# A two-layer graph attention kernel: loads, first products, copies and norms in other places at both ends

## The chip, the core and the metric

The kernel runs on one core of a Trainium2 chip. The metric is the device time of one execution in microseconds (us); less is better. TensorE (PE) multiplies, VectorE (DVE), ScalarE (ACT) and GpSimd (POOL) do the elementwise work, SyncE (SP) issues most of the DMAs. Each engine works through its own queue in order and waits on semaphores for the others.

## What is computed

The input `x` is 128 graphs of 128 nodes with 512 features, float32; `adj` is a boolean mask for each graph. Two layers follow each other, each a masked attention with a residual sum and a layer norm:

```python
# layer 0: 4 heads of 64
x = layernorm(x + attention(x @ Wq, x @ Wk, x @ Wv, mask=adj) @ Wo + bo)
# layer 1: 8 heads of 64, with a layer norm of its own ahead, the diagonal always allowed
h = (x - mean(x)) * rsqrt(var(x) + 1e-5) * gamma + beta
q, k, v = split(h @ w_qkv.T)
x = layernorm(x + attention(q, k, v, mask=adj | eye) @ w_out.T + b_out)
```

`attention` is softmax(q k' / 8, masked) v for each head.

## The kernel before

The 128 graphs are worked in 64 groups `g` of two. The whole program is unrolled, and the order of the source is the order of each engine's queue. `opening` loads and turns the weights and starts groups 0 and 1; `step(s)` for s = 2 to 63 works on several groups at once, layer 0 of group s beside layer 1 of groups s-3 to s-5; `closing_a` (s = 64), `closing_b(65)`, `closing_b(66)` and `last` (s = 67) empty this pipeline.

The matrix products are done by Strassen's scheme (Winograd's form): 2x2 blocks, seven products numbered 1 to 7, with sums of the blocks made beforehand. `sums` and `out_sums` (both through `halves_sums`, L323) make those of the activations on POOL with four subtractions or additions, `combine` (L206) those of the weights on DVE. Products 1, 6, 7, 4 accumulate in one PSUM bank `a`, 5 and 3 in `f`, 2 goes into `c`. In between, the bank is read: after 1, 5 and 6 by a copy on ACT ("tap", L369 and L499), after the others by an addition on DVE. So product 6 of a kind waits for the tap of 1, 7 for that of 6, 4 for the addition of 7.

- `product_0` (L461) makes q, k and v of layer 0 from `xT` and `w0`; `qk` and `v` (`product`, L331) those of layer 1; `out_product` (L507) the output projections, with their additions into the rows `R` at L532.
- Attention: `scores` (L544, part 0 for layer 0, parts 1 and 2 for the two graphs of layer 1), `masked` (L585, copies of the allowed scores into `SM` on DVE), `maxima` (L599), `exps` (L606, eight on ACT in two halves), `normalised` (L615, a reciprocal on DVE and a product on POOL), then the turn of the probabilities: `blocks` (L633) transposes 32x32 blocks on DVE and writes them to a scratch in DRAM, `probs_arrive` fetches them back into `pT` by four DMAs; `blocks_direct` (L654) turns them on PE instead. `attend` (L668) multiplies them with v and copies the result to `aT` on ACT. `cleared` (L578) fills `SM` with the masking value on POOL.
- Rows: `addend` (L706) adds the bias to `R` on POOL (for layer 1 after a scaling on ACT, L712), `stats` (L718) takes mean and variance on DVE, `roots` computes scale and shift on POOL and puts the norm itself into a list `later`; `flush()` emits what stands there: two ACTIVATEs (L758) and, for layer 1, the output DMA. `finish_direct` (L295) turns the rows for layer 1 on PE.
- `setup` is a list of weight turns (four PE transposes each and a copy to SBUF), filled by `load_transposed` and emitted by `prepare(n)`.
- At the very end `out_plain` makes the last two output rows, graph by graph, in plain products, each graph in a bank of its own with two halves; `norm_plain` adds, takes the statistics and normalises.

SP issues the loads in source order. Wq is loaded by ACT's queue, Wk and Wv by SP's, w_qkv and w_out last. In steps 3 and 4 the tap-free product 2 of v is put ahead of product 1 (L936).

Of the kernel before, what the change touches and what calls it, by code (L numbers as in the profile page):

```python
# [27 lines left out]
def kernel(ctx: ExitStack, tc: tile.TileContext, x, adj, wq, wk, wv, wo, bo,  # L28
# [87 lines left out]


    ident = const.tile([P, P], F32, name="ident")
    make_identity(nc, ident)
    eye = const.tile([P, P], U8, name="eye")  # L120
    nc.vector.tensor_copy(eye, ident)
    mhalf = const.tile([P, 4], F32, name="mhalf")
    nc.gpsimd.memset(mhalf, -0.5)


    HF = INNER[0] // 2
    w0 = const.tile([P, KC, 3, 2, HF], F32, name="w0")
    ws0 = const.tile([P, 3, KC // 2, 3, HF], F32, name="ws0")
# [20 lines left out]
    gb_raw = one.tile([2 * KC, P], F32, tag="sm2", name="gb_raw")  # L149
    gb = const.tile([P, 2 * KC], F32, name="gb")  # L150

    setup = []
    def load_transposed(dst, src, name):
        rows, cols = src.shape
        raws = []
        for r in range(rows // P):
            raw = spare.pop(0)
            nc.sync.dma_start(raw, src[r * P:(r + 1) * P, :])
            raws.append(raw)

        def part(r):
            raw = raws[r]
            pt = mm_tile(f"{name}t_{r}")
            for c in range(cols // P):
                nc.tensor.transpose(pt[:, c * P:(c + 1) * P], raw[:, c * P:(c + 1) * P], ident)
# [7 lines left out]
        setup.extend(lambda r=r: part(r) for r in range(rows // P))  # L173

    nc.sync.dma_start(gb_raw[:KC], gamma.rearrange("(c p) -> c p", p=P))
# [7 lines left out]


# [23 lines left out]
    def weight_sums_0():  # L208
        combine(*(w0[:, c:c + KH, :, h] for c in (0, KH) for h in range(2)), *(ws0[:, i] for i in range(3)))
# [85 lines left out]
    def finish_direct(g):  # L295
# [13 lines left out]
        sums(1, g)  # L309
# [21 lines left out]
    def product(kind, g, i, take=True):  # L331
# [17 lines left out]
        elif first:  # L349
            ACC[kind, which] = ps_st.tile([P, 512], F32, tag=which, name=f"{kind}{which}_{g}")  # L350
# [110 lines left out]
    def product_0(g, *which):  # L461
# [6 lines left out]
        for i in which:  # L468
# [4 lines left out]
            bank, first = INTO[i]  # L473
            if first and bank == "c":
# [14 lines left out]
            for n, (o, lhsT, rhs) in enumerate(todo):  # L489
                nc.tensor.matmul(o, lhsT, rhs, start=first and n == 0, stop=n == len(todo) - 1,  # L490
                                 skip_group_check=True)
            src = acc[:, :3 * P]
# [291 lines left out]
    def norm_plain(g, b):  # L784
        row = R[g][:, b]
        n = E // 2
        acc = ACC["op", b]
        st = two.tile([P, 2, nc.vector.BN_STATS_DIM], F32, tag="st_last", name=f"st_last{b}")
        for i in range(2):
            h = slice(i * n, (i + 1) * n)  # L790
            nc.vector.tensor_add(row[:, h], acc[:, h], row[:, h])
# [5 lines left out]
        nc.gpsimd.tensor_tensor(root, ve, mhalf[:, :1], op=ALU.pow)  # L797
        nc.vector.tensor_scalar(row, row, mv[:, 0:1], root, op0=ALU.subtract, op1=ALU.mult)
        nc.sync.dma_start(out[g * G + b], row)


# [13 lines left out]
    def opening():  # L815
# [4 lines left out]
        for h in range(2):  # L820
            nc.scalar.activation(w0[:, :, 0, h, :], w0[:, :, 0, h, :], AF.Copy, scale=SCALE)
        product_0(0, 1)
        weight_sums_0()
        product_0(0, 2, 5, 6, 3)
# [31 lines left out]
    def step(s):  # L856
# [26 lines left out]
        normalised(s, 0)  # L883
        out_product(0, s - 2, *(() if s == 2 else (6,)), 3)
        exps(s, 1, 0)
# [77 lines left out]
    def closing_a():  # L963
# [31 lines left out]
        blocks(s, 1)  # L995
        exps(s, 2, 1)
# [151 lines left out]
```

## Time and profile before

| | us |
|---|---|
| median of 3 runs | 2765.82 |
| lowest and highest | 2763.13, 2767.58 |
| the profiled execution | 2759.03 |
| its span, first to last instruction | 2757.3 |
| PE, DVE, ACT, POOL busy outside 200 to 2600 us | 328, 229, 169, 200 |

The profile is that of one execution. A line of its timeline has start, duration, engine, source line, operation, output and inputs, the shape and the number of merged records; in square brackets stand the idle time of the engine before it and what ended that. "issue" means a time in which an engine waited for nothing that is shown. A float32 matmul leaves two records. The lines of who waits for whom give the total, the number of waits and the longest. The granted TensorE clock was 0.999 over the execution.

### The profile page before, as it was taken

Reading aid. Unit: us, or ns where it says so; the run is one execution under the profiler, and the core shown is the slowest. Engines: PE = TensorE matmul, PEld = TensorE weight load, DVE = VectorE, ACT = ScalarE, POOL = GpSimd, SP = SyncE. Lnnn points to the kernel's source line nnn. Section 1 sums busy time; section 2 is a strip of 40 time slices with the busy share of each in tenths; the row PEclk is TensorE's granted clock in tenths of the full one; section 3 lists DMA queues with packets and bytes.
Section 4 is the critical chain, followed back from the end, with each engine's and each line's share of the span. In section 5 each row is a group of like instructions: output and inputs, shape, how many; then the busy total and the mean of one; then the engine's idle time right before and its main releaser. Section 6 shows DMA issues by size and latency. Waiting matters only on the chain.

```text
span 2757.3 us, 49223 instructions
## 1 busy us (share of the span) xinstructions
PE 2725.2 (99%) x15781; PEld 2024.6 (73%) x15781; DVE 2025.0 (73%) x3662; ACT 1510.6 (55%) x4805; POOL 1750.2 (63%) x2311
## 2 busy tenths in 40 slices
PE   8999999999999999999999999999999999999998
PEld 7867777677776677776776766777767767677787
DVE  5777777777777777777777777777777777777665
ACT  3465565564564655655645546556556465465554
POOL 4566666666666666666666666666666666666664
PEclk9999999999999999999999999999999999999999
DMA  6577878778778788787787787877877877878741
GB/s 171 151 196 211 220 205 222 209 205 225 214 202 227 202 215 218 206 220 213 202 228 209 208 224 203 218 212 207 225 207 207 225 206 214 219 204 222 204 126 62
DMA packets 525330, 562.73 MB, mean 204 GB/s; under 512 B 55304, under 2 KB 434192, under 8 KB 525072
## 3 DMA queue, kind: packets, MB, share of 16 engines
q1 hardware_dynamic: 524496, 559.05, 75.8%
q8 instruction: 127, 2.08, 0.3%
q14 instruction: 131, 1.07, 0.1%
q10 hardware_dynamic: 576, 0.52, 0.1%
HBM read 300.95 MB, written 258.47 MB: 203 GB/s over the span
## 4 chain that ended last, share of the span: by engine, by line
PE 89%; DMA 4%; ACT 3%; DVE 1%; POOL 1%; SPq 1%; issue 1%; ACTq 0%; POOLq 0%; DVEq 0%
PE qka L359 14%; PE a L490 11%; PE oa L528 11%; PE va L359 8%; PE qkf L359 7%; PE av L691 6%; PE of L528 6%; PE f L490 5%; PE vf L359 4%; PE qkc L359 4%; PE c L490 3%; PE oc L528 3%; PE sc L562 2%; PE sc L568 2%; PE vc L359 2%; DMA scrk<-tk 2%
## 5 line engine op out<-in xcount | busy, mean ns | idle before, releaser
L612 ACT ACTIVATE sm<-sm,nmax 128x128 f32<-128x128 f32 x1536 | 595.4, 393 | 7.6 <-DVE nmax L603 6.0
L621 POOL TENSOR_TENSOR sm<-sm,rec 128x1024 f32<-128x1024 f32 x192 | 364.1, 1896 | 360.5 <-DVE rec L620 357.6
L713 POOL TENSOR_TENSOR r<-r,bias 128x1024 f32<-128x1024 f32 x128 | 301.4, 2356 | 127.1 <-ACT r L712 127.1
L532 DVE TENSOR_TENSOR r<-oa,r 128x256 f32<-128x256 f32 x508 | 211.5, 416 | 159.8 <-PE oa L528 126.0
L612 ACT ACTIVATION_READ_ACCUMULATOR sm<-sm,nmax 128x1 f32 x1536 | 295.4, 192 | 0.0
L369 ACT COPY ev<-va 128x256 f32<-128x256 f32 x128 | 47.6, 372 | 442.9 <-PE va L359 442.9
L732 POOL TENSOR_SCALAR ve<-mv 128x2 f32<-128x2 f32 x191 | 41.4, 217 | 376.8 <-DVE mv L725 366.3
L639 DVE STREAM_TRANSPOSE turnedp<-sm 128x1024 f32<-128x1024 f32 x188 | 233.4, 1242 | 63.8 <-POOL sm L621 63.8
L758 ACT ACTIVATE r<-r,shift,root 128x512 f32<-128x512 f32 x254 | 192.8, 808 | 122.2 <-POOL shift L747 122.2
L603 DVE TENSOR_REDUCE nmax<-sm 128x8 f32<-128x1024 f32 x192 | 226.3, 1204 | 0.1
L359 PE MATMUL qkf<-w,xs 128*128 128x512 f32 x472 | 221.8, 592 | 0.0
L359 PE MATMUL qka<-wsqk,xs 128*128 128x512 f32 x472 | 221.8, 592 | 0.0
L528 PE MATMUL oa<-wso,so 128*128 128x256 f32 x760 | 206.1, 380 | 2.3 <-POOL so L323 1.8
L528 PE MATMUL of<-wo,so 128*128 128x256 f32 x760 | 206.0, 380 | 0.7 <-POOL so L323 0.4
L323 POOL TENSOR_TENSOR xs<-xT 128x256 f32<-128x256 f32 x256 | 188.3, 736 | 28.3 <-DVE xT L112 23.4
L490 PE MATMUL a<-ws,xs 128*128 128x128 f32 (+1 forms) x760 | 182.1, 375 | 0.0
L490 PE MATMUL f<-w,xs 128*128 128x128 f32 (+1 forms) x760 | 182.1, 375 | 0.0
L597 DVE COPY_PREDICATED sm<-m,sc 128x512 f32<-128x512 uint8 x256 | 172.5, 727 | 12.1 <-PE sc L562 3.6
L724 DVE BATCH_NORM_STATS2 st<-r 128x6 f32<-128x512 f32 x254 | 174.9, 688 | 2.3
L583 POOL MEMSET sm<- 128x1024 f32 x192 | 174.9, 952 | 0.0
L359 PEld LDWEIGHTS qka<-wsqk,xs 128*128 128x128 f32 x472 | 89.7, 190 | 112.9 <-issue 112.9
L359 PEld LDWEIGHTS qkf<-w,xs 128*128 128x128 f32 x472 | 89.7, 190 | 112.9 <-issue 112.9
(181 smaller groups left out, 6478.6 us busy)
## 6 DMA issues: line engine op xcount, KB each, us to landing
scrp<-turnedp SPq DMA_DIRECT2D x188, 512.0 KB, 3.2
pT<-scrp SPq DMA_DIRECT2D x252, 256.0 KB, 5.2
x<-in_x_dram SPq DMA_DIRECT2D x256, 128.0 KB, 5.0
r<-in_x_dram SPq DMA_DIRECT2D x64, 512.0 KB, 3.2
out_dram<-r SPq DMA_DIRECT2D x63, 512.0 KB, 4.3
scr<-turned SPq DMA_DIRECT2D x62, 512.0 KB, 4.7
raw<-scr SPq DMA_DIRECT2D x248, 128.0 KB, 4.1
pT<-scrp SPq DMA_DIRECT2D x248, 128.0 KB, 3.9
```

Source lines behind the costliest of these rows:

```text
L323: nc.gpsimd.tensor_tensor(o, a0, a1, op=op)
L359: nc.tensor.matmul(o, lhsT, rhs, start=first and m == 0, stop=m == len(todo) - 1, skip_group_check=True)
L490: nc.tensor.matmul(o, lhsT, rhs, start=first and n == 0, stop=n == len(todo) - 1, skip_group_check=True)
L528: nc.tensor.matmul(acc, left[:, c], right[:, c], start=first and c == 0, stop=c == hk - 1, skip_group_check=True)
L532: nc.vector.tensor_add(part, acc, part)
L583: nc.gpsimd.memset(sm, NEG1 if part else NEG0)
L603: nc.vector.tensor_reduce(NMAX[part], SM[part], AX.X, ALU.max, negate=True)
L612: nc.scalar.activation(sm[:, i, k, :], sm[:, i, k, :], AF.Exp, bias=nmax[:, i, k:k + 1], accum_out=total[:, i, k:k + 1])
L621: nc.gpsimd.tensor_tensor(SM[part], SM[part], rec[:, :, :, None].to_broadcast([P, 2, K1, N]), op=ALU.mult)
L639: nc.vector.transpose(t.rearrange("p q (h r) -> p q h r", r=32), SM.pop(part).rearrange("p i k (q r) -> p q (i k) r", r=32))
L713: nc.gpsimd.tensor_tensor(R[g], R[g], (bias0, bias1)[l][:, None, :].to_broadcast([P, G, E]), op=ALU.add)
L758: nc.scalar.activation(R[g][:, b], R[g][:, b], AF.Identity, bias=shift[:, b:b + 1], scale=root[:, b:b + 1])
```

## The change

The first loads: the loader of Wq, Wk, Wv is a function, with Wv now on ACT's queue; the `eye` copy is on ACT; the loads of w_qkv's rows stand ahead of and between those of group 1's `x`, the masks, rows, `wo` and the biases. Twelve matmuls of the identity with itself stand at the head of PE's queue. Wq is scaled on DVE, and products 1 and 2 of group 0 as well as the sums of its weights are done for q, k and v one after the other. In steps 3 and 4 product 1 of v has another bank (`a0`) and its old order, and `normalised(s, 0)` stands later. In the closing turns masks, copies, norms, turns of blocks and clearings stand in other places of the queues. At the end the additions, statistics and norms of the two last graphs are interleaved. Nothing in `step` changes for s above 4.

```diff
+    HF = INNER[0] // 2
...
+    def load_w0(i, queue):
+        for a in range(4):
+            queue.dma_start(w0[32 * a:32 * a + 32, :, i].rearrange("p c h f -> p c (h f)"),
+                            (wq, wk, wv)[i][a * P:(a + 1) * P].rearrange("(c i) f -> i c f", i=32))
+    load_w0(0, nc.scalar)
     ident = const.tile([P, P], F32, name="ident")
     make_identity(nc, ident)
     eye = const.tile([P, P], U8, name="eye")
-    nc.vector.tensor_copy(eye, ident)
+    nc.scalar.copy(eye, ident)
...
-    for i, w in enumerate((wq, wk, wv)):
-        for a in range(4):
-            (nc.sync if i else nc.scalar).dma_start(
-                w0[32 * a:32 * a + 32, :, i].rearrange("p c h f -> p c (h f)"),
-                w[a * P:(a + 1) * P].rearrange("(c i) f -> i c f", i=32))
-    load_mask(0)
-    load_rows(0)
-    load(1)
-    wo0 = const.tile([P, INNER[0] // P, E], F32, name="wo0")
-    nc.sync.dma_start(wo0, wo.rearrange("(c p) f -> p c f", p=P))
-    bias0 = const.tile([P, E], F32, name="bias0")
-    nc.sync.dma_start(bias0, bo[None, :].to_broadcast([P, E]))
-    bias1 = const.tile([P, E], F32, name="bias1")
-    nc.sync.dma_start(bias1, b_out[None, :].to_broadcast([P, E]))
-    transposed(0)
-    load_quarters(1)
+    load_w0(1, nc.sync)
+    load_w0(2, nc.scalar)
+    ready = mm_tile("ready")
+    for _ in range(12):
+        nc.tensor.matmul(ready[:, :P], ident, ident, start=True, stop=True, skip_group_check=True)
...
+    def load_transposed(dst, src, name, *which):
...
+        for r in which:
+            raw = spare.pop(0)
+            nc.sync.dma_start(raw, src[r * P:(r + 1) * P, :])
+            setup.append(lambda r=r, raw=raw: part(r, raw))
+    transposed(0)
+    load_transposed(w1, w_qkv, "w_qkv", 0, 1, 2, 3)
+    load_quarters(1)
+    load_mask(0)
+    load_transposed(w1, w_qkv, "w_qkv", 4, 5)
+    wo0 = const.tile([P, INNER[0] // P, E], F32, name="wo0")
+    nc.sync.dma_start(wo0, wo.rearrange("(c p) f -> p c f", p=P))
+    load_transposed(w1, w_qkv, "w_qkv", 6, 7, 8, 9)
+    load_rows(0)
+    bias0 = const.tile([P, E], F32, name="bias0")
+    nc.sync.dma_start(bias0, bo[None, :].to_broadcast([P, E]))
+    load_transposed(w1, w_qkv, "w_qkv", 10, 11)
...
+    setup.append(turn_gamma_beta)
+    load_transposed(wo1, w_out, "w_out", 0, 1, 2, 3)
+    setup.append(setup.pop(-3))
+    load(1)
+    bias1 = const.tile([P, E], F32, name="bias1")
+    nc.sync.dma_start(bias1, b_out[None, :].to_broadcast([P, E]))
...
-    def weight_sums_0():
-        combine(*(w0[:, c:c + KH, :, h] for c in (0, KH) for h in range(2)), *(ws0[:, i] for i in range(3)))
+    def weight_sums_0(t):
+        combine(*(w0[:, c:c + KH, t, h] for c in (0, KH) for h in range(2)), *(ws0[:, i, :, t] for i in range(3)))
...
-    load_transposed(w1, w_qkv, "w_qkv")
-    setup.append(turn_gamma_beta)
-    load_transposed(wo1, w_out, "w_out")
-    setup.append(setup.pop(-3))
...
-        sums(1, g)
...
         elif first:
-            ACC[kind, which] = ps_st.tile([P, 512], F32, tag=which, name=f"{kind}{which}_{g}")
+            own = kind == "v" and g < 2 and which == "a"
+            ACC[kind, which] = ps_st.tile([P, 512], F32, tag="a0" if own else which, name=f"{kind}{which}_{g}")
...
-    def product_0(g, *which):
+    def product_0(g, *which, ts=(0, 1, 2)):
...
             bank, first = INTO[i]
+            first = first and 0 in ts
...
             if g in PLAIN_0:
                 todo = [(parts[:, (t + odd) % 3], *((right[:, c, t], left[:, c]) if t < 2 else
                                                     (left[:, c], right[:, c, t])))
-                        for t in range(3) for c in range(KH)]
+                        for t in ts for c in range(KH)]
...
+            if 2 not in ts:
+                continue
...
-    def norm_plain(g, b):
-        row = R[g][:, b]
+    def add_plain(g, b, i):
         n = E // 2
-        acc = ACC["op", b]
-        st = two.tile([P, 2, nc.vector.BN_STATS_DIM], F32, tag="st_last", name=f"st_last{b}")
-        for i in range(2):
-            h = slice(i * n, (i + 1) * n)
-            nc.vector.tensor_add(row[:, h], acc[:, h], row[:, h])
-            nc.vector.bn_stats(st[:, i], row[:, h])
-        mv = two.tile([P, nc.vector.BN_AGGR_DIM], F32, tag="mv", name=f"mv_last{b}")
-        nc.vector.bn_aggr(mv, st)
+        h = slice(i * n, (i + 1) * n)
+        row = R[g][:, b, h]
+        if i == 0:
+            ST[b] = two.tile([P, 2, nc.vector.BN_STATS_DIM], F32, tag="st_last", name=f"st_last{b}")
+        nc.vector.tensor_add(row, ACC["op", b][:, h], row)
+        nc.vector.bn_stats(ST[b][:, i], row)
+        mv = MV["last", b] = two.tile([P, nc.vector.BN_AGGR_DIM], F32, tag="mv", name=f"mv_last{b}")
+        nc.vector.bn_aggr(mv, ST[b])
         ve, root = (two.tile([P, 1], F32, tag=t, name=f"{t}_last{b}") for t in ("ve1", "root1"))
         nc.gpsimd.tensor_scalar(ve, mv[:, 1:2], 1.0, EPS, op0=ALU.mult, op1=ALU.add)
         nc.gpsimd.tensor_tensor(root, ve, mhalf[:, :1], op=ALU.pow)
+        return root
+    def norm_plain(g, b, root):
+        row, mv = R[g][:, b], MV["last", b]
         nc.vector.tensor_scalar(row, row, mv[:, 0:1], root, op0=ALU.subtract, op1=ALU.mult)
         nc.sync.dma_start(out[g * G + b], row)
...
         for h in range(2):
-            nc.scalar.activation(w0[:, :, 0, h, :], w0[:, :, 0, h, :], AF.Copy, scale=SCALE)
-        product_0(0, 1)
-        weight_sums_0()
-        product_0(0, 2, 5, 6, 3)
+            nc.vector.tensor_scalar_mul(w0[:, :, 0, h, :], w0[:, :, 0, h, :], SCALE)
+        for t in range(3):
+            product_0(0, 1, 2, ts=(t,))
+            weight_sums_0(t)
+        product_0(0, 5, 6, 3)
...
-        normalised(s, 0)
+        if s not in (3, 4):
+            normalised(s, 0)
         out_product(0, s - 2, *(() if s == 2 else (6,)), 3)
+        if s in (3, 4):
+            normalised(s, 0)
...
-        if s in (3, 4):
-            second = product("v", s - 3, 2, take=False)
-            v(s - 3, 1)
-            second()
-        else:
-            v(s - 3, 1, 2)
+        v(s - 3, 1, 2)
...
         blocks(s, 1)
+        cleared(s + 1, 1)
         exps(s, 2, 1)
...
         stats(1, s - 5, 1)
-        cleared(s + 1, 1, 2)
+        cleared(s + 1, 2)
         with_self(s - 2)
-        blocks(s, 0)
-        probs_arrive(s, 0)
-        addend(0, s - 1)
-        addend(1, s - 4)
...
     def closing_b(s):
         made = scores(s, 1, 2)
-        masked(made, s, 1, 2)
+        masked(made, s, 1)
+        if s == NG + 1:
+            blocks(s - 1, 0)
+            probs_arrive(s - 1, 0)
+            addend(0, s - 2)
+            addend(1, s - 5)
+        maxima(s, 1)
         v(s - 4, 1, 2)
-        maxima(s, 1)
+        flush()
         v(s - 4, 6, 5)
         exps(s, 1, 0)
-        flush()
         v(s - 4, 7, 3)
-        maxima(s, 2)
+        masked(made, s, 2)
         v(s - 4, 4)
-        exps(s, 1, 1)
-        normalised(s, 1)
         attend(s, 1, 2)
         out_sums(1, s - 5)
-        blocks(s, 1)
+        exps(s, 1, 1)
+        maxima(s, 2)
         finish_direct(s - 3)
+        normalised(s, 1)
         out_product(1, s - 5, 1, 2)
         attend(s, 0)
         out_sums(0, s - 2)
         exps(s, 2, 0)
+        blocks(s, 1)
         out_product(1, s - 5, 5, 6)
+        sums(1, s - 3)
+        exps(s, 2, 1)
         qk(s - 3, 1)
-        exps(s, 2, 1)
+        normalised(s, 2)
         out_product(1, s - 5, 7, 3)
         qk(s - 3, 2)
-        normalised(s, 2)
         out_product(1, s - 5, 4)
-        qk(s - 3, 6)
         blocks(s, 2)
         probs_arrive(s, 1, 2)
+        cleared(s + 1, 1, 2)
+        qk(s - 3, 6)
         out_product(0, s - 2, 1, 2, 5)
         qk(s - 3, 5)
...
         out_product(0, s - 2, 7)
+        flush()
         qk(s - 3, 3)
         out_product(0, s - 2, 4)
-        cleared(s + 1, 1, 2)
         qk(s - 3, 4)
...
         out_plain(NG - 1, 1, 0, 1)
-        norm_plain(NG - 1, 0)
-        norm_plain(NG - 1, 1)
+        for i in range(2):
+            add_plain(NG - 1, 0, i)
+        root = root_plain(0)
+        add_plain(NG - 1, 1, 0)
+        norm_plain(NG - 1, 0, root)
+        add_plain(NG - 1, 1, 1)
+        norm_plain(NG - 1, 1, root_plain(1))
```

More of the change, by code (lines that the diff above doesn't have):

```diff
@@ L115 @@
     load_quarters(0)
+    HF = INNER[0] // 2
+    w0 = const.tile([P, KC, 3, 2, HF], F32, name="w0")
+    ws0 = const.tile([P, 3, KC // 2, 3, HF], F32, name="ws0")
+    def load_w0(i, queue):
[3 more added lines that the diff above has]
+    load_w0(0, nc.scalar)
     ident = const.tile([P, P], F32, name="ident")
@@ L120, with part @@
     eye = const.tile([P, P], U8, name="eye")
-    nc.vector.tensor_copy(eye, ident)
+    nc.scalar.copy(eye, ident)
     mhalf = const.tile([P, 4], F32, name="mhalf")
     nc.gpsimd.memset(mhalf, -0.5)
-    HF = INNER[0] // 2
-    w0 = const.tile([P, KC, 3, 2, HF], F32, name="w0")
-    ws0 = const.tile([P, 3, KC // 2, 3, HF], F32, name="ws0")
-    for i, w in enumerate((wq, wk, wv)):
-        for a in range(4):
-            (nc.sync if i else nc.scalar).dma_start(
-                w0[32 * a:32 * a + 32, :, i].rearrange("p c h f -> p c (h f)"),
-                w[a * P:(a + 1) * P].rearrange("(c i) f -> i c f", i=32))
-    load_mask(0)
-    load_rows(0)
-    load(1)
-    wo0 = const.tile([P, INNER[0] // P, E], F32, name="wo0")
-    nc.sync.dma_start(wo0, wo.rearrange("(c p) f -> p c f", p=P))
-    bias0 = const.tile([P, E], F32, name="bias0")
-    nc.sync.dma_start(bias0, bo[None, :].to_broadcast([P, E]))
-    bias1 = const.tile([P, E], F32, name="bias1")
-    nc.sync.dma_start(bias1, b_out[None, :].to_broadcast([P, E]))
-    transposed(0)
-    load_quarters(1)
+    load_w0(1, nc.sync)
[3 more added lines that the diff above has]
+        nc.tensor.matmul(ready[:, :P], ident, ident, start=True, stop=True, skip_group_check=True)
     w1 = const.tile([P, KC, 3 * INNER[1]], F32, name="w1")
     wo1 = const.tile([P, INNER[1] // P, E], F32, name="wo1")
-    gb_raw = one.tile([2 * KC, P], F32, tag="sm2", name="gb_raw")
-    gb = const.tile([P, 2 * KC], F32, name="gb")
     setup = []
[L153 to L162, printed above, removed]
+    def load_transposed(dst, src, name, *which):
+        def part(r, raw):
             pt = mm_tile(f"{name}t_{r}")
-            for c in range(cols // P):
+            for c in range(KC):
                 nc.tensor.transpose(pt[:, c * P:(c + 1) * P], raw[:, c * P:(c + 1) * P], ident)
@@ L171, in part @@
                 nc.vector.tensor_copy(to, pt)
-        setup.extend(lambda r=r: part(r) for r in range(rows // P))
+        for r in which:
[14 more added lines that the diff above has]
+    load_transposed(w1, w_qkv, "w_qkv", 10, 11)
+    gb_raw = one.tile([2 * KC, P], F32, tag="sm2", name="gb_raw")
+    gb = const.tile([P, 2 * KC], F32, name="gb")
     nc.sync.dma_start(gb_raw[:KC], gamma.rearrange("(c p) -> c p", p=P))
@@ L782, in out_plain, with root_plain @@
                                  stop=c == K1 - 1, skip_group_check=True)
[L784 to L785 removed]
+    def add_plain(g, b, i):
         n = E // 2
[L787 to L794 removed]
+        h = slice(i * n, (i + 1) * n)
[4 more added lines that the diff above has]
+        nc.vector.bn_stats(ST[b][:, i], row)
+    def root_plain(b):
+        mv = MV["last", b] = two.tile([P, nc.vector.BN_AGGR_DIM], F32, tag="mv", name=f"mv_last{b}")
+        nc.vector.bn_aggr(mv, ST[b])
         ve, root = (two.tile([P, 1], F32, tag=t, name=f"{t}_last{b}") for t in ("ve1", "root1"))
@@ L797, in norm_plain @@
         nc.gpsimd.tensor_tensor(root, ve, mhalf[:, :1], op=ALU.pow)
+        return root
+    def norm_plain(g, b, root):
+        row, mv = R[g][:, b], MV["last", b]
         nc.vector.tensor_scalar(row, row, mv[:, 0:1], root, op0=ALU.subtract, op1=ALU.mult)
         nc.sync.dma_start(out[g * G + b], row)
+    ST = {}
     def v(g, *which):
```

## The prediction

> **What bounds the kernel now.** I read the page first, then the busy time by stage, then who TensorE (PE) waits for at the two ends, then the timeline around each wait.
>
> ```profile
> span 2757.3 us, 49223 instructions
> ...
> PE 2725.2 (99%) x15781; PEld 2024.6 (73%) x15781; DVE 2025.0 (73%) x3662; ACT 1510.6 (55%) x4805; POOL 1750.2 (63%) x2311
> ```
>
> The reader is to see that PE is busy in all but 32.1 us of the span; no other engine passes 73%. The stages say where those 32 us are:
>
> ```profile
> 200.00:1000.00 800.00, 798.25 (x4493) 583.54 (x4492) 598.37 (x1082) 446.68 (x1424) 516.41 (x680) 1.00 0.80 213
> 1000.00:2600.00 1600.00, 1598.74 (x8964) 1165.71 (x8963) 1197.19 (x2162) 894.62 (x2849) 1033.88 (x1368) 1.00 0.80 213
> ```
>
> The first number after the length is PE's busy time: 3.0 us idle in 2400. The steady loop has nothing to give; all that can be had lies in the first 130 us and after 2600. PE's waits there, first of the opening, then of the closing:
>
> ```profile
> PE a L490 <- ACT w L821: 10.1, 1, 10.1
> PE w_qkvt L165 <- DMA raw_r<-in_L_gnn_w_qkv_dram: 1.5, 1, 1.5
> PE va L359 <- ACT ev L369: 1.0, 2, 0.5
> PE a L490 <- DMA w<-in_L_gnn_Wv_dram: 0.9, 1, 0.9
> PE oa L528 <- DVE r L532: 0.4, 1, 0.4
> ```
>
> ```profile
> PE oa L528 <- ACT aT L696: 2.7, 2, 1.6
> PE oa L528 <- POOL so L323: 1.8, 2, 1.1
> PE av L691 <- DMA pT<-scrp: 1.5, 1, 1.5
> PE qka L359 <- ACT xT L289: 1.0, 1, 1.0
> PE va L359 <- DVE v L384: 0.6, 1, 0.6
> PE of L528 <- POOL so L323: 0.4, 1, 0.4
> ```
>
> Each wait is short, so a fix is worth at most its own length. One loss hides inside "busy": the same eight records at 10 us and at 28 us.
>
> ```profile
> 10.07 2.08 PE L490 MATMUL a<-xT,w 128*128 128x128 f32 x8 [10.07 <-ACT w L821]
> 28.24 1.16 PE L490 MATMUL a<-xT,w 128*128 128x128 f32 x8
> ```
>
> 0.26 us a record against 0.13 (pitch 0.111: twelve start at 28.24 and the next product at 29.57). The first 24 records run from 10.07 to 16.36; at the later pitch they would take 2.7.
>
> [...] full speed comes near 15.7 us, 5.6 after the start; no row shows how long a warm array stays warm. [...] So I give Wv on ACT's queue no earlier arrival than the trace shows (issues at 6.95 to 8.8, last landing 12.8). [...] the first sum of `op_0` waits until the whole bank is written (the tail's rows below), not just its half.
>
> **Opening, in order of time.** x's last quarter lands near 8.3 (transposes start at 8.38 and end at 9.69), Wq at 8.04. Before, ACT loads its table (1.28) and scales half 0 by 10.0. After, the table load moves to the `eye` copy, beside the loads, and DVE scales behind the transposes: two TENSOR_SCALARs of 128x512, nearest row L798 at 0.55 (I bound it by 0.3 and 0.6). PE's start becomes 9.69 + 0.55 = 10.25, a loss of 0.2. The 12 identity matmuls are 24 records; from `ident` (1.3) at the cold 0.26 they end by 7.6, before x, and so cost nothing. They should leave the array warm[...].
>
> Products 1 and 2 now go in three parts of 8 records (0.89 warm). q: 10.25 to 11.15; k (Wk landed by 10.4): to 12.05; v waits for Wv, 13.0 to 13.9. DVE: the sums are four 128x256 subtractions for each part, 0.43 each by the L206 row, 1.72: q 10.8 to 12.5, k to 14.2, then product 2's addition (behind ACT's copy) to 15.2, v to 16.9 with its first result at 15.65. Product 5 does 8 records to 14.8, waits 0.85, ends at 16.1; products 6 and 3 at 1.33 each end at 18.8 (20.54 before). The setup turns wait for `raw_r`, issued at 17.99 before; now the first four go right behind the projection weights, about 9 to 11, and with 3.8 to land are long there. Turns 0.9, product 7 1.33, turns 0.9, product 4 1.34: scores(1) begin at 23.4, against 26.96. **Gain 3.5; I take 3.4.** If the array is cold again (0.26 until about 15.7), the same sum gives 24.6, **2.3**.
>
> Every transfer of the SP queue is reordered, so who is late next? By the stages the DMA moved 1.72 MB in the first 10 us and 3.01 in the next. Ahead of and including x(1), mask 0, w_qkv 4 and 5 and wo stand 4.5 MB, there by 20; x(1) is wanted at 23.4, the rest at 24 to 28. Rows 0 and bias0 (6.3 MB, at the 366 GB/s of 20 to 30 us near 24.3) are wanted by `addend` at 36.47 - 3.5 = 33. load(1) and bias1 go last and are wanted after 39. x(1)'s WAR wait on the transposes (9.69) holds up nothing that is due. The cover is some 4 us for x(1) and 9 for the rows.
>
> Steps 3 and 4: v's first product gets bank a0, so 1 can precede 2 and 6 no longer waits for the copy (0.52 each): **1.0**. Bank a0 is next wanted by scores, 1.0 us after v(4) ends; its copy takes 0.37. `normalised(s, 0)` behind two additions removes L532's 0.44: **0.4**.
>
> **closing_b(65)**, scores at 2650.84. `masked` of part 2, behind v's additions, removes the 0.63. aT's copies move ahead of four exps: the 1.04 goes. `out_sums(1)` ahead of `normalised(1)` on POOL removes the 0.68. The early `cleared(66, 1)` sits in a POOL idle of 2.56 at 2643. But part 0's turn now follows `masked`: its write goes out at 2654.95 instead of 2654.06 (SP was held by the fetches until then). It landed at 2660.1, behind 1 MB of fetches, and will still; the fetch of pT 0 lands near 2665.4, while PE is ready for `attend(0)` at 2663.9. A wait of 1.5 takes the old ones' place; attend(0) starts at 2665.4 instead of 2665.92. Behind it 0.68 is saved, and ht and the first products no longer push: qk(1) at 2668.2 instead of 2669.69. **Gain 1.5.** The flush now ahead of v(6) puts 1.5 us of norms on ACT (2654.4 to 2655.9) before the tap that v(7) needs at 2656.4: covered with 0.1 to spare.
>
> **closing_b(66).** The waits 1.61, 0.43 and 1.14, 3.18 in all, go by the same moves and because one pair of norms (1.5 us of ACT) is flushed a step early, behind out_product(0), where ACT idles 3 to 4 us. New: on DVE `blocks(1)` stands ahead of the additions of products 5 and 6. In us from this step's scores: aT copied at 10.9, POOL's four sums (0.72) to 13.85, `normalised` 1.9 to 15.75, turn 1.25 to 17.05, additions to 17.85; out_product 7 accumulates into that bank and is ready at 16.9. A wait of 1.0 is born. **Net 2.2.** The second pair of exps, no longer behind qk(1)'s tap, ends at 17.0; POOL does part 2's `normalised` at 18.7 to 20.6, and its turn, behind product 4's addition, starts at 23.0 (26.9 before), so that the write of pT's source goes out some 4 us earlier.
>
> **last().** The 1.5 us wait for pT shrinks to 0 to 0.4 (write 24.3, landing 3.2, four issues 1.7, landing 5: 34.4, wanted at 34.4); POOL's `normalised(1)` is then late by 0.25. **Net 1.1.**
>
> **Tail.** Before:
>
> ```profile
> 2747.46 0.42 DVE L791 TENSOR_TENSOR r<-op,r 128x256 f32<-128x256 f32 x1 [4.25 <-PE op L781]
> ...
> 2750.84 0.42 DVE L791 TENSOR_TENSOR r<-op,r 128x256 f32<-128x256 f32 x1
> ...
> 2753.71 0.55 DVE L798 TENSOR_SCALAR r<-r,mv_last,root_last 128x512 f32<-128x512 f32 x1 [0.96 <-POOL root_last L797]
> ```
>
> PE's first half of op_0 ended near 2745.4, yet the addition began at 2747.46, when the bank was complete. So `add_plain(1, 0)`, now ahead of `norm_plain(0)`, will hold DVE until PE's end (2750.8), and the 0.55 of norm 0 falls between the two additions of b = 1: **loss 0.6**. Were the wait by halves, it would be a gain of 0.75.
>
> **Sum:** 3.4 + 1.0 + 0.4 + 1.5 + 2.2 + 1.1 - 0.6 = 9.0. Against the profiled execution's span 2757.3 that is 2748.3 (2750.0 with the 1.7 outside the span, 2759.03 before). The median shown is 2765.82, 6.8 above that execution; I carry the difference over: **2756.8**.
>
> **Rivals.** (a) *The waits change places.* A cold array (2.3), attend(0) no earlier at all (0), 66's new wait doubled (1.2), pT still late (0), steps 1.4, tail -0.6: 4.3 gained, 2761.5. For it: each wait has another just behind it, pT 0 lands with under 1 us of slack. Against: two of the three new waits are counted above already. (b) *No new waits:* opening 3.5, steps 1.5, closing 2.35 + 3.18 + 1.25, tail +0.75: 12.5, 2753.3. For it: my queue sums are rough by 0.5 us each[...]. (c) *Slower: the reordered loads leave the loop's DMA issues out of step.* SP's issue of Wk waited 3.0 us on landings of Wq, which it doesn't read, so an issue can wait for an unrelated earlier one. If a new order makes fetches late in each of the 59 steps from s = 5 on, 0.15 us a step eats the whole gain; at 0.25 the loss is 59 x 0.25 = 14.8 and the net 14.8 - 9.0 = 5.8 slower, 2771.6. For it: DMA share 0.80. Against: number and order of the loop's transfers stay the same, and PE has no fetch wait there now. (d) That the identity matmuls do nothing is the cold case, within (a).
>
> **Numbers.** Forecast 0.54, (a) 0.23, (b) 0.16, (c) 0.07. A measurement of this kernel can tell about 0.2%, 5.5 us, from no change. The forecast and (b) lie beyond it: faster 0.70; (a) within: same 0.23; (c): slower 0.07. The range runs from below (b)'s value, 2752.5, to 2763, which takes in (a) and leaves out (c).
>
> **What would show it.** First product at 10.2 with 8 records in about 1.1 us (warm); scores(1) near 23.4; no wait for `raw_r`; the v waits of step 3 and 4 gone; in the closing PE waiting for pT 0 about 1.5 and for DVE's r about 1.0; DVE's last TENSOR_SCALAR some 3.9 to 4.1 us after PE's end (3.4 before). The forecast is wrong if the stages between 200 and 2600 gain PE idling, or if x(1) or rows 0 appear as a PE wait.

## The result, and the profile after

Six executions of each kernel, on the same chip: before 2765.98 us in the median (2763.13 to 2769.26), changed 2756.80 (2754.01 to 2758.58); ratio 0.9966, 95% interval 0.9954 to 0.9978. The gain is 9.2 us, 0.34%. The profiled execution of the changed kernel took 2755.1, only 3.9 less than that of the kernel before (2759.03); where those 5 us went has to be told too.

The page and the windows of the loop in the changed kernel:

```profile
span 2753.3 us, 49277 instructions
...
PE 2729.1 (99%) x15805; PEld 2029.4 (74%) x15805; DVE 2026.2 (74%) x3671; ACT 1509.7 (55%) x4804; POOL 1750.8 (64%) x2311
...
200.00:1000.00 800.00, 797.27 (x4492) 583.40 (x4491) 598.53 (x1082) 445.61 (x1422) 516.80 (x683) 1.00 0.79 213
1000.00:2600.00 1600.00, 1596.81 (x8958) 1164.35 (x8957) 1193.86 (x2159) 892.31 (x2846) 1031.14 (x1362) 1.00 0.79 213
```

PE idles 24.2 us of the span instead of 32.1; but 4.75 us of its busy time are now the identity matmuls, which compute nothing that is wanted. In the unchanged loop it idles 5.9 us of 2400 instead of 3.0. Who PE waits for at the two ends (0 to 200 us, then from 2590 on):

```profile
PE a L490 <- DMA w<-in_L_gnn_Wv_dram: 4.1, 2, 3.9
PE ready L138 <- POOL mhalf L132: 1.3, 1, 1.3
PE a L490 <- DVE qkv L506: 0.9, 2, 0.5
...
PE pt L665 <- POOL sm L623: 0.3, 1, 0.3
PE of L530 <- POOL so L321: 0.2, 1, 0.2
...
```

```profile
PE oa L530 <- DVE rec L622: 1.4, 1, 1.4
PE av L693 <- DVE sm L599: 1.0, 1, 1.0
PE av L693 <- DMA pT<-scrp: 0.6, 1, 0.6
...
```

Gone are the 1.5 for `raw_r`, the two of v's tap, and in the closing those for `aT`, `so` and v. The 10.1 for Wq's scaling only look different: they are now 1.34 and 3.92 us of idling with the identity matmuls in between, and the first product starts at 10.01 instead of 10.07. The profile puts the 3.92 down to Wv, which that product doesn't read; it starts when DVE has scaled the first half of Wq (9.57 to 9.95). New are the waits for `rec` and for `sm`, those for `qkv` in steps 3 and 4 (0.32 and 0.54), and two of step 2 for POOL's `so` and `sm` (0.23 and 0.30). The opening on PE's timeline:

```profile
1.34 4.75 PE L138 MATMUL ready<-ident 128*128 128x128 f32 x24 [1.34 <-POOL mhalf L132]
10.01 1.22 PE L490 MATMUL a<-xT,w 128*128 128x128 f32 x4 [3.92 <-DMA w<-in_L_gnn_Wv_dram]
...
13.98 1.23 PE L490 MATMUL a<-w,xT 128*128 128x128 f32 x4 [0.19 <-DMA w<-in_L_gnn_Wv_dram]
15.00 0.80 PE L490 MATMUL c<-w,xT 128*128 128x128 f32 x4
15.64 1.06 PE L490 MATMUL f<-xs,w 128*128 128x128 f32 x8
...
24.64 1.35 PE L564 MATMUL sc<-qkv 64*128 64x128 f32 x16
```

The reader is to see the pace: four records last 1.22 us at 10.01, eight last 1.06 at 15.64. The identity matmuls end at 6.09, PE idles 3.92 us, and product 1 starts on a cold array. The granted TensorE clock, third from the end in a line by stretches, says the same: full from 5.16 to 8.57, then half until 15.40.

```profile
5.16:8.57 3.41, 0.93 (x8) 0.74 (x7) 0.23 (x1) 0.00 (x0) 0.00 (x0) 1.00 1.16 210
8.57:15.40 6.83, 5.20 (x22) 4.91 (x23) 6.61 (x12) 0.15 (x1) 4.15 (x5) 0.50 1.10 281
```

`scores(1)` begin at 24.64 instead of 26.96.

By stages, each from one group of PE's records to the next (opening and steps from the span's start to the scores of step 5, the others from the scores on `kt` of one turn to those of the next):

| stage | before | changed | gain |
|---|---|---|---|
| to scores(1) | 26.96 | 24.64 | 2.32 |
| scores(1) to scores(5) | 105.53 | 104.78 | 0.75 |
| loop, scores(5) to `closing_a` | 2490.0 | 2494.7 | -4.7 |
| `closing_a` to turn 65 | 29.3 | 28.7 | 0.7 |
| turn 65 | 37.07 | 35.68 | 1.39 |
| turn 66 | 33.67 | 31.34 | 2.33 |
| `last()` to the product `op` | 21.06 | 19.48 | 1.58 |
| `op` to the end | 13.67 | 14.06 | -0.39 |

Without the loop it is 8.7 us.

### The profile page after: what moved, and what is told of

Read it like the earlier page. It is cut to its first block, busy times and chain, and to the rows that moved or that the text cites. A ratio compares the mean times of both kernels' runs of the same rounds, so it can differ in the third digit from the quotient of the medians.

```text
span 2753.3 us, 49277 instructions
## 1 busy us (share of the span) xinstructions
PE 2729.1 (99%) x15805; PEld 2029.4 (74%) x15805; DVE 2026.2 (74%) x3671; ACT 1509.7 (55%) x4804; POOL 1750.8 (64%) x2311
## 4 chain that ended last, share of the span: by engine, by line
PE 84%; DMA 7%; ACT 4%; DVE 2%; SPq 2%; issue 1%; POOL 0%; ACTq 0%; POOLq 0%; DVEq 0%
PE qka L358 13%; PE a L490 11%; PE oa L530 10%; PE va L358 7%; PE qkf L358 7%; PE av L693 6%; PE of L530 5%; PE f L490 5%; PE vf L358 3%; PE qkc L358 3%; DMA scrk<-tk 3%; PE c L490 3%; PE sc L564 3%; PE oc L530 2%; PE sc L570 2%; ACT sm L614 2%
```

## The experiments

**Does the loop lose what the opening gains?** Both kernels were profiled once more, unchanged, and the change was cut in two: `opening_only` has the changed opening and steps 3 and 4 with the old closing turns and tail, `closing_only` the reverse.

> The kernel before, profiled once more. Its loop, from the scores of step 5 to the first of closing_a's scores on kt, took 2490.0 us in the first profile, and 2494.7 to 2498.9 in the five profiles of kernels with the changed opening. Theory A (the loop varies from one execution to the next, whatever the opening): now 2493 to 2500, with 5 to 10 us of PE waits between 130 and 2590 us instead of 2.8. Rival (c) of the forecast (the new order of loads costs the loop some 5 us): 2490 +- 1 again, and a span near 2757.

> The changed kernel, profiled once more. Theory A: its loop lies somewhere in 2490 to 2500 (2494.7 before), while the stages outside it agree within 0.5 us with those of its first profile. Rival (the loop's length belongs to the kernel): 2494.7 +- 0.5.

> The changed opening and steps 3 and 4, with the closing turns, last() and the tail of the kernel before. Theory A (the gains add): 3.1 us below before by the stages, ratio 0.9989; scores of step 5 at 129.4 and the stages from closing_a on as long as before. Rival B (the loop waits for transfers and gives back what the opening gains): ratio 1.000.

> The opening and steps of the kernel before, with the changed closing turns, last() and tail. Theory A (the gains add): 5.9 us below before by the stages, ratio 0.9979; with opening_only's ratio it makes 0.9967. Rival B (the opening gives nothing): all of it is here, ratio 0.9966.

The second profile of the kernel before, PE's waits from 130 to 2590 us:

```profile
PE va L359 <- DVE tk L405: 4.7, 12, 1.1
PE sc L562 <- ACT qkv L277: 2.1, 4, 1.0
```

These are 6.8 us where the first profile had 2.8, on the same two waits; its loop took 2496.0 us, 6.0 more, and its execution 2765.56, 6.5 more. `closing_only`, whose loop is fed by the old opening too, took 2500.1. So the old opening gives 2490 to 2500. Kernels with a changed opening gave 2494.7, 2496.1 and 2497.8 (three profiles of the changed kernel) and 2494.3 to 2498.9 in eight others. The loop varies by some us from one execution to the next, whatever stands ahead of it; why stays open. The first profile of the kernel before had caught a short one: its 2759.03 lie below all 55 timed executions of that kernel (lowest 2763.13). Rival (c) falls. The stages outside the loop are steadier, but not all within the 0.5 us expected: in `after_again` turn 65 took 36.95 and `closing_a` 29.4. `scores(1)`, too, began at 24.64, 25.16 and 24.95 in the three profiles of the changed kernel, and at 24.31 in `opening_only`, whose opening is the same.

Timed, over 21 executions each: `opening_only` 0.9981 (0.9974 to 0.9987), which is 5.3 us (3.6 to 7.2) of 2766.56; `closing_only` 0.9983 (0.9977 to 0.9990), 4.7 us (2.8 to 6.4). The product is 0.9964, the whole change 0.9966: the halves add. The stages of the first pair of profiles say 3.1 and 5.6; the first lies just below its interval, so that the 0.9989 expected of `opening_only` was missed, and where the other 0.5 us or more of the opening's gain comes from stays open.

**What holds the opening?** Four kernels change the opening of the changed kernel: `o_none` has no `ready` matmuls, `o_28` and `o_28_sp` have 28, `o_28_sp` loads Wv from SP besides, and `o_whole` alone has products 1 and 2 whole again. The edits of `o_28_sp`, then of `o_whole`:

```diff
-    load_w0(2, nc.scalar)
+    load_w0(2, nc.sync)
...
-    for _ in range(12):
+    for _ in range(28):
```

```diff
-        for t in range(3):
-            product_0(0, 1, 2, ts=(t,))
-            weight_sums_0(t)
-        product_0(0, 5, 6, 3)
+        product_0(0, 1)
+        for t in range(3):
+            weight_sums_0(t)
+        product_0(0, 2, 5, 6, 3)
```

> Changed kernel without the identity matmuls. Theory A (the 3.9 us of idling behind them let the array fall back, so they do nothing): the first four records of product 1 still take 1.2 us, scores(1) begin at 24.6 +- 0.2. Rival B (they shorten what is left of the warming up: full speed came 5.0 us after product 1's start, 5.6 in the kernel before): scores(1) about 0.6 later, 25.2. In the unchanged loop, from the scores of step 5 to those of closing_a, both say nothing new; if its length differs by some us from the changed kernel's 2493.7, the loop varies from run to run.

> 28 identity matmuls instead of 12: at 0.11 us a record once warm they end near 9.6, just ahead of product 1. Theory A (clock and then Wv): the first four records take some 0.5 us, PE then idles for Wv, which lands at 14.0 as before, and DVE's subtractions for v start near 15.8 instead of 16.4: scores(1) at 24.1, a gain of 0.5. Rival B (the clock alone cost what the forecast missed): scores(1) at 23.4. Rival C (the clock doesn't depend on these): 24.6.

> 28 identity matmuls, and Wv issued by SP right behind Wk instead of by ACT. Theory A (what is left is Wv's landing, which is late because ACT issues it from 5.6 to 9.4): issues end near 9.0, landing near 13.0, scores(1) at 23.3 to 23.5, the warm forecast. Rival B (the landing is set by the traffic, not by the issue): Wv lands at 13.9 again, scores(1) at 24.1. Rival C: what stands behind Wv on SP (w_qkv's first rows, 1.9 us later) becomes a wait of PE at 20 us.

> Changed kernel, but product 1 whole ahead of the subtractions and product 2 whole behind them, as before the change; load order and identity matmuls as changed. Theory A (the parts fill the time until Wv lands): product 2 comes whole behind Wv, product 5 starts near 16.5 instead of 15.6, scores(1) at 25.4; the other 1.5 of the opening's gain is the order of the loads. Rival B (DVE's subtractions set the pace either way): 24.6 +- 0.2.

`scores(1)` began at 24.53 in `o_none`, 23.95 in `o_28`, 23.87 in `o_28_sp`, 26.98 in `o_whole`. Each of these is one profile, and one and the same opening gave 24.31 to 25.16 above: differences of a few tenths are to be believed only where the timeline shows their cause. (The 2493.7 in the expectation of `o_none` is a slip for 2494.7.) Twelve identity matmuls gain nothing, as theory A has it; the last section shows that they can even cost something. PE in `o_28`:

```profile
1.34 9.24 PE L138 MATMUL ready<-ident 128*128 128x128 f32 x56 [1.34 <-POOL mhalf L132]
10.42 0.61 PE L490 MATMUL a<-xT,w 128*128 128x128 f32 x4
...
13.67 0.71 PE L490 MATMUL a<-w,xT 128*128 128x128 f32 x4 [1.30 <-DMA w<-in_L_gnn_Wv_dram]
...
16.16 0.71 PE L490 MATMUL f<-w,xs 128*128 128x128 f32 x4 [0.43 <-DVE w L211]
```

Without a gap ahead of it, product 1 runs at 0.45 us for four records (10.42 to 10.87), but 1.30 of what it saves is spent waiting for Wv: `scores(1)` come 0.69 earlier than in the changed kernel, near theory A's 0.5. (With 28 they run until 10.58, a little too long: product 1 starts 0.4 later than with twelve.) Then Wv on SP lands 1.0 us earlier and no wait for `raw_r` comes of it, but the theory that this was all that was left is wrong: 23.87 instead of 23.3 to 23.5. PE in `o_28_sp`:

```profile
12.66 0.68 PE L490 MATMUL a<-w,xT 128*128 128x128 f32 x4 [0.72 <-DMA w<-in_L_gnn_Wv_dram]
...
16.08 0.71 PE L490 MATMUL f<-w,xs 128*128 128x128 f32 x4 [1.34 <-DVE w L211]
```

The microsecond has moved to the wait of product 5 for DVE's subtraction. DVE in that kernel:

```profile
9.45 1.26 DVE L829 TENSOR_SCALAR w<-w 128x512 f32<-128x512 f32 x2
10.74 0.83 DVE L211 TENSOR_TENSOR w<-w 128x256 f32<-128x256 f32 x1
11.61 0.83 DVE L211 TENSOR_TENSOR ws<-w 128x256 f32<-128x256 f32 x1
12.47 0.83 DVE L211 TENSOR_TENSOR ws<-ws,w 128x256 f32<-128x256 f32 x1
13.23 0.41 DVE L211 TENSOR_TENSOR ws<-w,ws 128x256 f32<-128x256 f32 x1
```

Three of the subtractions take 0.83 instead of 0.42; POOL's four sums of x stand beside them (9.6 to 13.0). `o_whole` is 2.3 us later than the changed kernel, more than the 0.8 expected: product 5 too ran cold there (its first eight records 1.92 us, the granted clock half until 19.6), and PE had stood still for 1.79 us in product 1, waiting for Wv. So on a cold array the parts are worth as much as the whole gain of the opening (what they are worth on a warm one, no run shows), and with whole products the new order of the loads bought nothing by 27 us (26.98 against 26.96), although its `raw_r` wait is gone.

**The other stages, and a better kernel.** `all_a` changes five stages, the opening in three places.

```diff
-    load_w0(2, nc.scalar)
+    load_w0(2, nc.sync)
...
-    for _ in range(12):
+    for _ in range(22):
...
-            nc.vector.tensor_scalar_mul(w0[:, :, 0, h, :], w0[:, :, 0, h, :], SCALE)
+            nc.scalar.activation(w0[:, :, 0, h, :], w0[:, :, 0, h, :], AF.Copy, scale=SCALE)
...
-        if s not in (3, 4):
+        if s != 3:
             normalised(s, 0)
         out_product(0, s - 2, *(() if s == 2 else (6,)), 3)
-        if s in (3, 4):
+        if s == 3:
             normalised(s, 0)
...
+        probs_arrive(s, 1)
         blocks(s, 2)
-        probs_arrive(s, 1, 2)
+        probs_arrive(s, 2)
         qk(s - 3, 3)
...
-        blocks(s, 1)
+        if s == NG + 1:
+            blocks(s, 1)
         out_product(1, s - 5, 5, 6)
+        if s == NG + 2:
+            blocks(s, 1)
...
-            ACC["op", b] = ps_st.tile([P, 512], F32, tag=("a0", "f0")[b], name=f"op_{b}")
+            ACC["op", b] = (ps_st.tile([P, 512], F32, tag=("a0", "f0")[b], name=f"op_{b}"),
+                            mm_tile(f"op_{b}h"))
...
```

> The changed kernel with one edit in each of five stages, read stage by stage. Opening: 22 identity matmuls, Wv on SP behind Wk, ACT instead of DVE scales Wq. Theory (with a warm array and Wv at 12.7, DVE's chain of scales and subtractions is what sets the pace; the scales, 1.25 us of it, go to ACT): scores(1) at 22.9 +- 0.3; rival (ACT's scales or the subtractions beside POOL take it back): 23.5 to 23.9. Step 4: normalised(4, 0) back in its old place. Theory (its new place holds up DVE and made the 0.54 wait at 109.4): scores(4) to scores(5) 35.5 instead of 36.1; rival: 36.1. Closing turn 65: part 1 of pT is fetched ahead of part 2's turn, so that half of the 1 MB lands earlier. Theory (the new wait ahead of attend(1, 2), 1.0 and 2.2 us in the two profiles, is for that fetch): 34.7 instead of 35.7 or 37.0; rival (it is for a PSUM buffer that masked(2) frees): no change. Closing turn 66: blocks(1) behind the additions of products 5 and 6. Theory (blocks(1) ahead of them made the 1.4 wait): 30.0 to 30.5 instead of 31.3; rival (the next wait takes its place): 31.3. Tail: each half of op in a bank of its own. Theory (the first addition waits for the whole bank): the first addition starts some 3.5 us earlier and the end is 0.6 to 1.3 closer to op's start than 14.1; rival (by halves it waits as long): 14.1.

Stage by stage. *Opening:* `scores(1)` at 23.31, 1.3 earlier, between theory (22.9) and rival (23.5); with DVE free at 9.57 its subtractions still take 0.83 to 0.94 beside POOL. Behind it steps 2 and 3 took 54.10 instead of 53.48: x of group 2 is late next, DVE waits 2.25 us for it before it transposes at 39.84, and PE then waits 0.80 for DVE's `r` at 46.84. In a second profile (`all_a_timed`) x came a microsecond earlier, and it was 53.29; in `pool_late`, below, 0.6 later, and it was 54.83. *Step 4:* 35.32 instead of 36.07, theory right.

*Turn 65:* 34.36 instead of 35.68, theory right. That the wait which the profile puts on `sm` is one for pT is also seen in `all_a` itself, first DVE, then PE:

```profile
2659.00 1.33 DVE L599 COPY_PREDICATED sm<-m,sc 128x512 f32<-128x512 uint8 x2
```

```profile
2659.41 1.97 PE L693 MATMUL av<-pT,v 128*64 128x128 f32 x32
```

`masked(2)` is two copies of 0.7 us. With the fetch early, `attend(1, 2)` starts before even the first of them has ended, so it doesn't wait for it.

*Turn 66:* 29.69 instead of 31.34, more than the theory had (30.0 to 30.5). The new wait of PE in the changed kernel, which the profile puts down to the reciprocal queued behind the additions; DVE in that kernel; and DVE in `all_a`, where the wait is gone:

```profile
2705.28 1.10 PE L530 MATMUL oa<-wso,so 128*128 128x256 f32 x4 [1.40 <-DVE rec L622]
```

```profile
2703.25 1.25 DVE L641 STREAM_TRANSPOSE turnedp<-sm 128x1024 f32<-128x1024 f32 x1 [2.27 <-POOL sm L623]
2704.42 0.39 DVE L534 TENSOR_TENSOR r<-of,r 128x256 f32<-128x256 f32 x1
2704.73 0.41 DVE L534 TENSOR_TENSOR r<-oa,r 128x256 f32<-128x256 f32 x1
```

```profile
2699.39 0.42 DVE L534 TENSOR_TENSOR r<-of,r 128x256 f32<-128x256 f32 x1 [0.30 <-PE of L530]
2700.25 0.42 DVE L534 TENSOR_TENSOR r<-oa,r 128x256 f32<-128x256 f32 x1 [0.44 <-PE oa L530]
2701.37 1.25 DVE L641 STREAM_TRANSPOSE turnedp<-sm 128x1024 f32<-128x1024 f32 x1 [0.70 <-POOL sm L623]
```

In the first DVE waits 2.27 us for POOL with the two additions queued behind the turn; in the second each addition follows its own product, and the turn loses nothing, since it waits for POOL either way: it starts 14.83 us after the step's scores in both. Against the kernel before, turn 66 is now 3.98 us shorter, though the three waits that went were 3.18 long by the profile. PE's busy time in it fell too, from 30.49 to 29.69: back to back, records overlap (a group of four that lasts 1.03 is followed by the next after 0.86), and at a wait they don't. So the prediction's "a fix is worth at most its own length" doesn't hold.

*Tail:* 12.88 instead of 14.06, theory right. The first addition in the changed kernel (op starts at 2739.24), and the first two in `all_a` (at 2735.82):

```profile
2743.06 0.42 DVE L793 TENSOR_TENSOR r<-op,r 128x256 f32<-128x256 f32 x1 [4.25 <-PE op L783]
```

```profile
2737.92 0.42 DVE L793 TENSOR_TENSOR r<-op,r 128x256 f32<-128x256 f32 x1 [2.52 <-PE op L783]
2739.58 0.42 DVE L793 TENSOR_TENSOR r<-op_0h,r 128x256 f32<-128x256 f32 x1 [0.77 <-PE op_0h L783]
```

With both halves in one bank the first addition comes 3.82 us after op's start, when the whole bank is written; with a bank for each half, 2.10. (The expectation's "3.5 us earlier" was wrong: 1.7, as the halves take.)

Last, `pool_late` is `all_a` with POOL's sums of x, and the clearing behind them, held until DVE has done q's four subtractions, and `all_a` and the changed kernel were timed side by side.

> The kernel all_a with POOL's four sums of x held until DVE's first four subtractions (q's) are done. Theory (a DVE subtraction takes 0.83 instead of 0.42 us while a POOL addition or subtraction runs beside it): all of q's four at 0.42 now, and the doubled ones are those of k and v that run beside POOL, 4 x 0.8 us from some 11.3 on; as many are doubled as before, so scores(1) stay within 0.4 of 23.3. Rival (the first subtractions of an execution are slow by themselves, or for the loads' traffic): q's still at 0.83.

> The kernel all_a once more, timed. By its stages it should be some 7.4 us below the changed kernel's first profile outside the loop: opening and steps to the scores of step 5 1.5, closing turn 65 1.3, turn 66 1.6, last() 0.9, tail 1.2, together 6.5 to 7.5. Theory: 2749.6 +- 1.5 where the changed kernel has 2756.8, ratio to before 0.994. Rival (the loop gives a part of it back): 0.995 to 0.9966.

> The changed kernel itself, timed beside all_a on the same chip. Theory: ratio to before 0.9966 as in the first measurement, which is also the product of opening_only's and closing_only's (0.9981 x 0.9983 = 0.9964).

DVE and POOL in `pool_late`:

```profile
10.82 0.42 DVE L211 TENSOR_TENSOR ws<-w,ws 128x256 f32<-128x256 f32 x1
...
11.61 0.42 DVE L211 TENSOR_TENSOR ws<-w 128x256 f32<-128x256 f32 x1
12.06 0.83 DVE L211 TENSOR_TENSOR ws<-ws,w 128x256 f32<-128x256 f32 x1
12.82 0.94 DVE L211 TENSOR_TENSOR ws<-w,ws 128x256 f32<-128x256 f32 x1
14.00 0.56 DVE L506 TENSOR_TENSOR qkv<-c,e 128x384 f32<-128x384 f32 x1 [0.24 <-ACT e L501]
```

```profile
11.64 0.98 POOL L321 TENSOR_TENSOR xs<-xT 128x256 f32<-128x256 f32 x1
...
14.31 0.73 POOL L321 TENSOR_TENSOR xs<-xT 128x256 f32<-128x256 f32 x1
```

The slow subtractions move with POOL: all four of q now take 0.39 to 0.43, and of those beside the sums three take 0.83, 0.94 and (at 14.47) 0.84. The fourth, at 11.61, started 0.03 ahead of POOL's first sum and took 0.42, and that sum took 0.98. `scores(1)` stay, at 23.16, since about as many are slowed as before; so this run shows what slows them, and not what that costs.

`all_a` took 2749.01 us (2748.67 to 2751.74, 5 executions), ratio to before 0.9943 (0.9930 to 0.9957), the changed kernel beside it 2756.46, 0.9967 (0.9954 to 0.9979). The ranges of the two don't overlap (the changed kernel's is 2755.01 to 2758.68). It beats both kernels, by 7.5 and 16.5 us, as the theory had it, though one term of that expectation was misread: `last()` takes 19.6 us in it, as in the changed kernel (19.5), not 0.9 less. By the means of three profiles each (with `pool_late` as the third of `all_a`), the 7.5 are 1.9 up to the scores of step 5, 1.8 in turn 65, 1.6 in turn 66 and 1.2 in the tail; a rest of about 1 lies within what the loop varies.

## Why the prediction was right

The time, 2756.8, is the forecast's, and so is the way: each wait that was to go went, and the three new ones that it named, for pT, behind `blocks(1)` and in the tail, are there, beside some in steps 2 to 4 that it did not name. But the agreement to 0.1 us is luck: by the stages of the first pair of profiles the opening and steps were forecast 1.7 us too high, the closing 1.4 too low. One of the signs of being wrong that it had named did appear, more idling of PE between 200 and 2600 us (5.9 instead of 3.0); but the kernel before idles 6.7 there in its second profile.

- *Opening, 3.4.* This is the step that failed: it was 2.3. "They should leave the array warm": by its own times PE was to idle 2.65 us behind them (7.6 to 10.25), and that so short a gap does no harm was an estimate of the author's that no row showed. 3.92 followed in the first profile, and the array was cold, the clock having gone to half at 8.57. But the length of the gap was not all that was wrong: in the two later profiles 2.96 followed, close to the forecast, and the array went cold as well, only a little later (at 10.4 and 10.8). It stayed warm where the identity matmuls ran up to product 1 (0 to 0.75 us of idling in five profiles). That the cold case's sum gave 24.6 exactly is chance, for the shortfall has two other terms. Of the 1.24 us between 23.4 and 24.64, by differences of single profiles, the clock is 0.69 (`o_28`), Wv's landing at 14.0 instead of 13.0 another 0.08 (`o_28_sp`, as long as DVE is behind it), and the rest, 0.47, are DVE's subtractions, priced 0.43 each and taking 0.83 beside POOL: v's first result was forecast for 15.65 and came at 16.03 in `o_28_sp`, and PE waited 1.34 for it. "No earlier arrival" for Wv on ACT's queue was right, and too kind: ACT issued from 5.6 to 9.4, 3.8 us for four, and it landed a microsecond later than by SP. Two readings were a little off: in the kernel before, the records keep the slow pace until 16.1, 6.0 us after the start, not until 15.7; and the product behind the twelve records of 28.24 starts at 29.68, not 29.57.
- *Loads.* The cover was there: no PE wait for x(1), rows 0 or a weight turn in the changed kernel. In `all_a`, 1.3 us earlier, x of group 2 is late.
- *Steps 3 and 4, 1.4.* Measured 1.14, 1.02 in step 3 and 0.12 in step 4; the stage's 0.75 is less because step 2 lost 0.38 to the two waits for POOL, which no term had and whose cause stays open. The v waits went (1.0). `normalised(s, 0)`, costed as a gain of 0.4, removed the 0.44 in step 3 (0.32 for `qkv` stands in its place there), but cost 0.75 in step 4, where there was no wait of `oa` to remove: with the old place step 4 takes 35.32. The wait that the move removes was priced; what is queued behind the moved instruction, in the step without that wait, was not.
- *Turn 65, 1.5.* Measured 1.39, with pT late as forecast, by 1.6 in all instead of 1.5, though in two waits, one of them for parts 1 and 2. That transfer has no margin: in three profiles of the changed kernel the gain was 1.4, 0.1 and 1.2.
- *Turn 66, 2.2.* Measured 2.33; the new wait behind `blocks(1)` is 1.4 instead of 1.0, and its cause is shown by `all_a`. Two errors cancel here: 3.18 less 1.4 would be 1.8, but taking the three waits out is worth 3.98.
- *`last()`, 1.1.* Measured 1.58; the wait for pT went wholly, not to 0 to 0.4.
- *Tail, -0.6.* Measured -0.39, for the reason given: the last TENSOR_SCALAR ends 3.92 us after PE, as forecast (3.9 to 4.1; 3.46 before). By halves it would have been a gain, and in `all_a` it is: 0.8 against the kernel before.
- *`closing_a`, nothing.* It gained 0.7 in this pair of profiles. Over three each it is 0.5, but the eight profiles with this `closing_a` took 28.6 to 31.9 in it and the three with the old one 29.0 to 29.8, so that no gain is shown.
- *The carry-over of the median.* Adding the 6.8 us by which the profile of before lay below its median was right, and now has a reason: the loop of that execution was short by nearly as much (6.0 against the second profile).

## What to carry over

Matmuls that only keep the array warm paid here where they ran up to the first real product (`scores(1)` at 23.95 in `o_28`, at 24.53 with none): count the idle time behind them, not their number. Up to 0.75 us of it was harmless here and 2.96 was not; what lies between was not measured. An instruction moved past a wait in one step of a loop is to be priced in each step that it is moved in. Before a difference of a few us in a loop that nobody changed is explained, profile the same kernel twice.

## What the runs showed that was not expected

In the third profile of the changed kernel (`after_timed`) the array lost its clock after work had come again. PE idled only 2.96 us, and the first four records ran warm (0.55 us to the next start), the next ones cold (0.95):

```profile
1.34 5.49 PE L138 MATMUL ready<-ident 128*128 128x128 f32 x24 [1.34 <-POOL mhalf L132]
9.79 0.71 PE L490 MATMUL a<-xT,w 128*128 128x128 f32 x4 [2.96 <-DMA w<-in_L_gnn_Wv_dram]
10.34 1.00 PE L490 MATMUL c<-xT,w 128*128 128x128 f32 x4
```

```profile
10.40:17.23 6.83, 6.44 (x29) 5.94 (x29) 5.84 (x12) 0.48 (x1) 3.33 (x4) 0.50 1.13 273
```

The full clock had been granted at 6.99, when the identity matmuls had just ended (6.83), and went at 10.40. In all five profiles with twelve of them (three of the changed kernel, `opening_only`, `o_whole`) it lasted 3.41 us from its coming, whenever the idling began, and PE was busy for 0.54 to 1.15 us of these. When it came back decided the opening: at 15.0 and 15.4 where it was lost at 8.2 and 8.6 (`scores(1)` at 24.31 and 24.64), at 17.2 and 17.6 where it was lost at 10.4 and 10.8 (24.95 and 25.16). Without identity matmuls it came at 15.9 (24.53). So in two of four profiles of one opening the twelve brought `scores(1)` 0.4 to 0.6 us later than in the one profile without them.

So 2.96 us of idling were enough here for the clock to go, and the 3.41 us at whose end it went were not idle throughout. Gaps of 0.67 in `o_28_sp` and of 0.27 to 0.75 in `all_a`, `all_a_timed` and `pool_late` cooled nothing: in `o_28_sp`, `all_a` and `pool_late` the four records behind them took 0.55, 0.52 and 0.52 us to the next start.

DVE's subtractions of two SBUF tiles took twice as long beside a POOL sum that had begun before them (0.83 for 0.42, up to 0.94 in `all_a` and `pool_late`). Not all that DVE did was slowed, and not beside all that POOL did: the addition out of PSUM at 14.00 in `pool_late` took its usual 0.56 beside a POOL sum, and subtractions beside POOL's memset (13.09 to 14.04 in the changed kernel) took 0.41. With one input, the second of Wq's two scalings took 0.95 beside a POOL sum and the first, begun before that sum, 0.38 (changed kernel, 9.87 and 9.57). POOL's sums took longer too, but by less: behind or under a subtraction that had begun, those of the opening took 0.79 to 0.98; the one at 14.31 in `pool_late`, which began ahead of its subtraction, took 0.73, as where none ran (26.29 to 28.63 in the changed kernel).
